# Turned features and attention weights in 512-byte pieces, with four blocks interleaved, in a graph-attention stack

## The chip, the core and the metric

The kernel runs on one core of one Trainium2 chip. The metric is the device time of one execution in microseconds (us); lower is better. The core has five engines that run side by side, each through its own list of instructions in order: TensorE (PE: matmuls, with weight loads shown as PEld), VectorE (DVE), ScalarE (ACT), GpSimd (POOL) and SyncE (SP), which here does nothing but issue transfers (DMAs). [...]

## What is computed

128 independent graphs of 128 nodes with 512 features each pass through four layers. Each layer adds a graph attention to its input and normalizes the rows. All arithmetic is float32. Cut to what matters here:

```python
# layer 1, for one graph: x is 128 x 512, mask is 128 x 128
def gat_layer(x, mask, W, a_src, a_dst, bias, concat):
    xl = (x @ W).reshape(B, N, H, F)
    asrc = jnp.einsum('bnhf,hf->bnh', xl, a_src)
    adst = jnp.einsum('bnhf,hf->bnh', xl, a_dst)
    e = jax.nn.leaky_relu(asrc[:, :, None, :] + adst[:, None, :, :], NEG_SLOPE)
    e = jnp.where(mask[..., None], e, NEG_INF)
    attn = jax.nn.softmax(e, axis=1)
    out = jnp.einsum('bsdh,bshf->bdhf', attn, xl)
    ...
h = elu(gat_layer(x, mask, W1, att_src1, att_dst1, b1, concat=True))    # 4 heads of 256
h = gat_layer(h, mask, W2, att_src2, att_dst2, b2, concat=False)        # 1 head of 512
x = layernorm(x + h)
```

Layer 0 mixes the rows with one head and no weight matrix. Layer 2 has a 512 x 512 weight matrix and 8 heads of 64. Layer 3 mixes with one head again.

## The kernel before

**The work of one graph.** The function `graph(g)` records one graph's work as some 170 operations (`Op`), each with an engine, an assumed cost, what it reads and what it writes. The nodes lie on the 128 partitions. TensorE contracts over partitions, so the features and the attention weights must be turned before it can take them.

**How something is turned (`turned`, lines 343 to 367).** VectorE transposes 32 x 32 blocks (line 348) into a buffer `zb`. One DMA writes it to a scratch tensor `scr` in memory (line 353). A second DMA reads it back so that the 32 x 32 blocks land on the right partitions. The count n says how many 128 x 128 blocks are turned at once: 4 for features of 512 and for four heads, 1 for a single head. In memory the order is block of 32 columns, then n, then 32 columns. There are two ways to read it back:

- With `moving=True` (line 358) each partition gets 4 pieces of n x 32 elements (512 bytes for n = 4). This is used for the four heads of layer 1 alone. Block h of the result is then four runs of 32 elements (the helper `parts`, line 532), and TensorE takes it as the moving operand (line 540).
- Otherwise (line 363) each partition gets 4 x n pieces of 32 elements, which is 128 bytes, so that each block is one run of 128 elements. TensorE takes it as the stationary operand, in a weight load: the features at line 453 (with `w1a` and with `wha`), two groups of four heads at line 585, and single heads at line 470.

Per graph there are five transfers of the kind n = 4 (features for layer 1, four heads of layer 1, features for layer 2, and the 8 heads of layer 2 in two groups) and three of the kind n = 1.

**TensorE's work in a graph.** Line 453 multiplies features by a weight matrix (`project`): 12 matmuls with 344 columns (`w1a`), 16 with 257 columns (`w2a`, whose stationary operand `hT` doesn't come from `turned`), and 8 with 264 columns (`wha`). Line 540 mixes the four heads of layer 1 in 8 matmuls, with the features as weights and the attention as moving operand. Line 585 mixes the 8 heads of layer 2, with the attention as weights and 64 columns streamed. Line 470 mixes a single head (3 times). Line 506 turns a mask.

**What sets the order.** `Pipeline.plan` is a planner that places the operations of one graph on a circle of `PERIOD = 24.7` us. For each operation it knows the assumed cost, an extra time until a transfer has landed, and latencies by engine (6 us for SP). It takes operations in the order of their earliest time, less 0.6 of the work that is left behind them, plus a random shift with a fixed seed, and places each at the first free time on its engine's circle. `Pipeline.run` then lays the same plan for all 128 graphs, one period apart, sorts everything by due time, and emits it. The times serve the order alone: [...] One graph's plan is some 18 periods long, so many graphs are in work at once. The planner also hands out buffers: all float32 buffers of 128, 512 or 1024 elements per partition come from common pools, with as many slots as the plan needs. The setup work (weights, their products with the attention vectors) is emitted among the first periods.

Of the kernel before, what the change touches and what calls it, by code (L numbers as in the profile page):

```python
# [16 lines left out]
P = 128  # L17
# [133 lines left out]
def tile_gat_stack(  # L151
# [25 lines left out]
    nc = tc.nc  # L177
    B, N, F = x.shape
    H1, FH = a1_src.shape
    HF = H1 * FH  # L180
    H2, FO = ah1.shape
# [48 lines left out]
    flat = "h f -> (h f)"  # L230
# [40 lines left out]
    for k in range(KF):  # L271
        for s in range(2):
            for h in range(H1):
                c, o = slice(h * FH, (h + 1) * FH), HF + s * H1 + h
# [39 lines left out]
    def graph(g):  # L314
        ops = []

        def op(engine, cost, emit, ins=(), outs=(), extra=0.0):
            ops.append(Op(engine, cost, emit, list(ins), list(outs), extra))
# [21 lines left out]
            ), [row], [db], 1.0 + 0.1 * nh)  # L340
            return db

        def turned(src, n, moving=False):

            zb, scr, out = Buf(f"zb{n}", [P, 4, n, 32]), Buf(f"scr{n}", [P, n * P]), Buf(f"pt{n}", [P, n, P])
            op("DVE", 0.12 + 0.133 * n, lambda: nc.vector.transpose(  # L348
                zb.ap.rearrange("p b h c -> p h b c"),
                src.ap.rearrange("p (h b c) -> p h b c", h=n, c=32) if len(src.shape) == 2  # L350
                else src.ap.rearrange("p h (b c) -> p h b c", c=32),
            ), [src], [zb])
            op("SP", 0.4, lambda: nc.sync.dma_start(
                out=scr.ap, in_=zb.ap.rearrange("p b h c -> p (b h c)")
            ), [zb], [scr], 0.2 * n)
            flat = lambda: scr.ap.rearrange("p f -> (p f)")
            if moving:
                op("SP", 0.6, lambda: nc.sync.dma_start(
                    out=out.ap.rearrange("p h i -> p (h i)").rearrange("p (q e) -> p q e", q=4),
                    in_=flat().rearrange("(q p e) -> p q e", q=4, p=P),  # L360
                ), [scr], [out], 1.0)
                return out
            op("SP", 0.65, lambda: nc.sync.dma_start(
                out=out.ap.rearrange("p h (q c) -> p h q c", q=4),
                in_=flat().rearrange("(q p h c) -> p h q c", q=4, p=P, h=n),
            ), [scr], [out], 1.5)
            return out

        class Col:
# [8 lines left out]
        def attend(db, h0, nh, src, mask, scaled=False):  # L378


            z, zz, nm, rs, ri = (Buf(f"{t}{nh}", s) for t, s in (
                ("z", [P, nh, P]), ("zz", [P, nh, P]), ("nm", [P, nh]), ("rs", [P, nh]),
                ("ri", [P, nh])))

            def prelu():
                for h in range(nh):
                    nc.scalar.activation(  # L387
                        z.ap[:, h, :], db.ap[:, h0 + h, :], AF.Prelu, bias=src(h0 + h), alpha=SLOPE
                    )

            def masked():
                for h in range(nh):
                    nc.vector.tensor_tensor_reduce(  # L395
                        out=zz.ap[:, h, :].rearrange("p (b a) -> p a b", b=4),
                        in0=z.ap[:, h, :].rearrange("p (a b) -> p a b", b=4),
                        in1=mask.ap.rearrange("p (a b) -> p a b", b=4), scale=-1.0, scalar=FMAX,
                        op0=ALU.add, op1=ALU.min, accum_out=nm.ap[:, h : h + 1],
                    )  # L400

            def exp():
                for h in range(nh):
                    nc.scalar.activation(  # L404
                        zz.ap[:, h, :], zz.ap[:, h, :], AF.Exp, bias=nm.ap[:, h : h + 1], scale=-1.0,
                        accum_out=rs.ap[:, h : h + 1],
                    )

            op("ACT", 0.08 + 0.293 * nh, prelu, [db, src.buf], [z])
            op("DVE", 0.08 + 0.225 * nh, masked, [z, mask], [zz, nm])  # L410
            op("ACT", 0.39 * nh, exp, [zz, nm], [zz, rs])
            op("DVE", 0.07, lambda: nc.vector.reciprocal(ri.ap, rs.ap), [rs], [ri])
            if scaled:
                op("POOL", 1.3, lambda: nc.gpsimd.tensor_mul(
                    zz.ap, zz.ap, ri.ap.unsqueeze(2).to_broadcast([P, nh, P])
                ), [zz, ri], [zz])
            return turned(zz, nh, moving=scaled), ri

        def norm(y, on_act=False):

# [23 lines left out]
        def project(xT, wa, nk, ncol, nchunk, t, evict):  # L444

            w = ncol // nchunk

            def chunk(c, ev):
                px = bank()
                cols = slice(c * w, (c + 1) * w)  # L450

                for k in range(nk):
                    op("PE", w * 4 / 2400 + 0.006, lambda k=k: nc.tensor.matmul(  # L453
                        px.ap[:, :w], lhsT=xT.ap[:, k, :], rhs=wa[:, k, cols],
                        start=(k == 0), stop=(k == nk - 1),
                    ), [xT] if k == 0 else [xT, px], [px])
                if ev == "DVE":
                    op("DVE", 0.11 + w / 960, lambda: nc.vector.tensor_copy(  # L458
                        t.ap[:, cols], px.ap[:, :w]), [px], [t])
                else:  # L460
                    op("ACT", 0.16 + w / 1200, lambda: nc.scalar.copy(  # L461
                        t.ap[:, cols], px.ap[:, :w]), [px], [t])

            for n, c in enumerate(reversed(range(nchunk))):
                chunk(c, evict[n])

        def mixed(pt, xv, width):

            pa = bank()
            op("PE", width * 4 / 2400, lambda: nc.tensor.matmul(  # L470
                pa.ap[:, :width], lhsT=pt.ap[:, 0, :], rhs=xv.ap[:, :width], start=True, stop=True
            ), [pt, xv], [pa])
            return pa

# [33 lines left out]
        pt, ri = attend(db, 0, 1, Col(sc0, 0, 1), m0)  # L508
        pa = mixed(pt, x0, F)
# [11 lines left out]
        xT = turned(x1, KF)  # L521
        xb = Buf("xb", [P, F])
        op("POOL", 1.25, lambda: nc.gpsimd.tensor_add(xb.ap, x1.ap, b2t), [x1], [xb])  # L523
        xl = Buf("xl1", [P, C1])
        project(xT, w1a, KF, C1, 3, xl, ["ACT"] * 3)
        db = spread(Col(xl, HF, H1), H1)
        pt, ri = attend(db, 0, H1, Col(xl, HF + H1, H1), m1, scaled=True)
# [1 line left out]

        e1, r1, hT = (Buf(t, [P, KH, P]) for t in ("e1", "r1", "hT"))  # L530

        def parts(b):
            return b.ap.rearrange("p h i -> p (h i)").rearrange("p (q h c) -> p q h c", q=4, h=H1)

        def block(c, pt=pt):
            pa = bank()

            for u in range(4):
                k = 4 * c + u
                op("PE", 0.225, lambda u=u, k=k: nc.tensor.matmul(  # L540
                    pa.ap[:, u * P : (u + 1) * P].rearrange("p (q c) -> p q c", q=4), lhsT=xl.ap[:, k * P : (k + 1) * P],
                    rhs=parts(pt)[:, :, k * P // FH, :], start=True, stop=True,
                ), [xl, pt, pa] if u else [xl, pt], [pa])
            half = lambda b: b.ap[:, 4 * c : 4 * c + 4, :].rearrange("p k i -> p (k i)")

            def biased(out, func):
                for u in range(4):
                    k = 4 * c + u
                    nc.scalar.activation(  # L549
                        out.ap[:, k, :], pa.ap[:, u * P : (u + 1) * P], func, bias=b1t[:, k : k + 1]  # L550
                    )

            op("ACT", 1.1, lambda: biased(e1, AF.Exp), [pa], [e1])
            op("ACT", 1.1, lambda: biased(r1, AF.Relu), [pa], [r1])
            op("DVE", 0.6, lambda: nc.vector.scalar_tensor_tensor(
                out=half(hT), in0=half(e1), scalar=-1.0, in1=half(r1), op0=ALU.add, op1=ALU.min
            ), [e1, r1], [hT])
# [8 lines left out]
        pt, ri = attend(db, 0, 1, Col(xl2, F + 1, 1), m1)  # L566
        pa = mixed(pt, xl2, F)
# [5 lines left out]
        xT = turned(x2, KF)  # L573
# [5 lines left out]
        def heads(q):  # L579
            pt, ri = attend(db, 4 * q, 4, Col(xl3, F + H2, H2), m2)  # L580
            pa = bank()

            for u in range(4):
                h = 4 * q + u
                op("PE", 0.225, lambda u=u, h=h: nc.tensor.matmul(  # L585
                    pa.ap[:, u * FO : (u + 1) * FO], lhsT=pt.ap[:, u, :],
                    rhs=xl3.ap[:, h * FO : (h + 1) * FO], start=True, stop=True,
                ), [pt, xl3, pa] if u else [pt, xl3], [pa])
            cols = slice(q * 4 * FO, (q + 1) * 4 * FO)
            op("DVE", 0.34, lambda: nc.vector.tensor_mul(  # L590
                x3.ap[:, cols].rearrange("p (h o) -> p h o", h=4),
                pa.ap[:, : 4 * FO].rearrange("p (h o) -> p h o", h=4),
                ri.ap.unsqueeze(2).to_broadcast([P, 4, FO]),
            ), [pa, ri], [x3])
# [11 lines left out]
        pt, ri = attend(db, 0, 1, Col(sc4, 0, 1), m3)  # L606
# [49 lines left out]
```

## Time and profile before

| what | us |
|---|---|
| median of 3 runs | 3197.62 (3196.52 to 3199.8) |
| the profiled execution | 3201.2 |
| its span, first to last instruction | 3199.3 |
| PE busy | 3073.7 (96%) |
| DVE busy | 3003.9 (94%) |
| ACT busy | 2444.6 (76%) |
| POOL busy | 1563.7 (49%) |

A group in the profile is one line, engine, operation and shape. Its columns are the count, the busy time in us and the mean ns of one, then the engine's idle time before it and who ended it. These groups are touched by the change:

```profile
L348 DVE STREAM_TRANSPOSE w<-w 128x512 f32<-128x512 f32 x640 | 446.0, 697 | 23.3 <-PE ps L540 9.1 <-PE ps L585 1.0 <-ACT w L435 1.0
L585 PEld LDWEIGHTS ps<-xl,w 128*128 128x128 f32 x2048 | 295.3, 197 | 104.2 <-issue 78.9 <-DVE mv L423 7.1 <-DVE sT L330 3.9
L585 PE MATMUL ps<-xl,w 128*128 128x64 f32 x2048 | 278.5, 271 | 25.4 <-DVE mv L423 9.9 <-DMA w<-scr 9.7 <-DVE sT L330 3.5
L540 PE MATMUL ps<-w,xl 128*128 128x128 f32 x2048 | 256.3, 278 | 0.1
L540 PEld LDWEIGHTS ps<-w,xl 128*128 128x128 f32 x2048 | 239.6, 192 | 0.8 <-ACT xl L461 0.3
```

The mean of one overlaps with its neighbours: the 12 passes of line 585 that follow each other begin far less than 271 ns apart. So the time that a kind of instruction takes from the engine is read from the distance between starts, or from the chain of waits, which gives each stretch to one owner.

The transfers, counted over the whole run:

```profile
DMA packets 1640373, 600.46 MB, mean 188 GB/s; under 512 B 1310464, under 2 KB 1490688, under 8 KB 1640016
q1 hardware_dynamic: 1636608, 589.44, 74.8%
```

The second line is the queue of SyncE's transfers: packets, MB, and the time that they took as a share of 16 DMA engines over the span.

### The profile page before, as it was taken

To read this page: it belongs to the slowest core of one execution; us is meant where nothing else is said; L and a number is where in the kernel's file an instruction comes from. 1 tells how busy PE (TensorE), PEld (TensorE's weight loads), DVE (VectorE), ACT (ScalarE), POOL (GpSimd) and SP (SyncE) were. 2 spreads that over 40 slices of the span, in tenths; PEclk is the share of its full clock that TensorE was granted. 3 is DMA by queue.
4 is the path that set the end of the run, shared out by engine and by line. 5 is a ranking of instruction groups with operands and counts; after the bars stand their busy time and mean duration, and the time that the engine had idled before them with its cause. 6 is when DMAs were issued, how large, how long until landed. Compare 5 with 4: busy or idle time off the path is not lost.

```text
span 3199.3 us, 60449 instructions
## 1 busy us (share of the span) xinstructions
PE 3073.7 (96%) x14212; PEld 2378.0 (74%) x14212; DVE 3003.9 (94%) x9976; ACT 2444.6 (76%) x8961; POOL 1563.7 (49%) x2328
## 2 busy tenths in 40 slices
PE   3999999999999999999999999999999999999974
PEld 1677777777777777777777777777777777777762
DVE  5768999999999999999999999999999999999885
ACT  1567888877878788788787887878878878788864
POOL 4334545555545455555455554545555545555334
PEclk9999999999999999999999999999999999999985
DMA  4467787777878777788787777777777787778774
GB/s 149 116 154 186 190 196 196 195 197 193 199 192 198 193 198 194 196 197 197 191 199 196 193 196 195 197 196 196 194 199 193 195 196 197 197 192 196 175 167 112
DMA packets 1640373, 600.46 MB, mean 188 GB/s; under 512 B 1310464, under 2 KB 1490688, under 8 KB 1640016
## 3 DMA queue, kind: packets, MB, share of 16 engines
q1 hardware_dynamic: 1636608, 589.44, 74.8%
q0 software_dynamic: 1936, 6.62, 0.6%
q8 instruction: 115, 1.88, 0.3%
q14 instruction: 242, 1.98, 0.2%
q10 hardware_dynamic: 1472, 0.53, 0.1%
HBM read 368.91 MB, written 227.48 MB: 186 GB/s over the span
## 4 chain that ended last, share of the span: by engine, by line
PE 93%; DVE 3%; DMA 2%; POOL 1%; ACT 1%; issue 1%; SPq 0%; ACTq 0%; POOLq 0%; DVEq 0%
PE ps L453 69%; PE ps L470 10%; PE ps L540 7%; PE ps L585 6%; DMA w<-scr 1%; DVE w L495 0%; PE ps L506 0%; DMA scr<-w 0%; ACT w L404 0%; DVE w L395 0%; DVE st L422 0%; DMA w_-1_4_139<-in_L_gnn_att_dst_dram 0%; POOL rd L427 0%; DVE w L348 0%; DVE w_-1_1_94 L266 0%
## 5 line engine op out<-in xcount | busy, mean ns | idle before, releaser
L453 PE MATMUL ps<-w2a,w 128*128 128x257 f32 x4096 | 953.2, 380 | 3.1 <-DVE xl L458 3.1
L453 PE MATMUL ps<-w1a,w 128*128 128x344 f32 x3072 | 917.2, 455 | 1.9 <-ACT w L549 0.9
L453 PEld LDWEIGHTS ps<-w2a,w 128*128 128x128 f32 x4096 | 758.3, 190 | 121.1 <-DVE xl L458 3.9
L453 PEld LDWEIGHTS ps<-w1a,w 128*128 128x128 f32 x3072 | 587.4, 191 | 348.6 <-issue 41.1
L404 ACT ACTIVATE w<-w,nm 128x128 f32<-128x128 f32 x1920 | 767.3, 412 | 31.9 <-DVE nm L395 26.6
L387 ACT ACTIVATE w<-w,xl 128x128 f32<-128x128 f32 x1664 | 543.5, 447 | 265.5 <-DVE w L513 239.6
L395 DVE CUSTOM_DVE_ANT_0 w<-w,w 128x128 f32<-128x128 f32 x1920 | 666.3, 456 | 24.7 <-ACT w L387 11.6
L549 ACT ACTIVATE w<-ps,b1t 128x128 f32<-128x128 f32 x2048 | 560.6, 404 | 112.3 <-PE ps L540 112.3
L348 DVE STREAM_TRANSPOSE w<-w 128x512 f32<-128x512 f32 (+1 forms) x1024 | 544.0, 541 | 32.3 <-PE ps L540 9.1
L426 POOL TENSOR_SCALAR rd<-mv 128x1 f32<-128x1 f32 x512 | 118.5, 232 | 920.5 <-DVE mv L423 894.3
L453 PEld LDWEIGHTS ps<-wha,w 128*128 128x128 f32 x2048 | 390.4, 191 | 121.4 <-issue 36.8
L453 PE MATMUL ps<-wha,w 128*128 128x264 f32 x2048 | 480.0, 388 | 0.0
L461 ACT COPY xl<-ps 128x344 f32<-128x344 f32 (+2 forms) x640 | 277.9, 435 | 175.3 <-PE ps L453 165.8
L404 ACT ACTIVATION_READ_ACCUMULATOR w<-w,nm 128x1 f32 x1920 | 401.2, 209 | 0.0
L523 POOL TENSOR_TENSOR w<-w,b2t 128x512 f32<-128x512 f32 x128 | 165.9, 1296 | 467.5 <-DVE w L348 282.0
L585 PEld LDWEIGHTS ps<-xl,w 128*128 128x128 f32 x2048 | 295.3, 197 | 104.2 <-issue 78.9
L422 DVE BATCH_NORM_STATS2 st<-w 128x6 f32<-128x512 f32 x512 | 353.9, 691 | 11.8 <-POOL w L614 7.3
L427 POOL TENSOR_TENSOR rd<-rd,neghalf 128x1 f32<-128x1 f32 x512 | 307.4, 600 | 42.7
L470 PE MATMUL ps<-w,w 128*128 128x512 f32 x512 | 281.7, 633 | 32.5 <-DMA w<-scr 16.1
L585 PE MATMUL ps<-xl,w 128*128 128x64 f32 x2048 | 278.5, 271 | 25.4 <-DVE mv L423 9.9
L395 DVE DVE_READ_ACCUMULATOR2_ANT nm<- 128x1 f32 x1920 | 291.4, 152 | 0.0
L495 DVE CUSTOM_DVE_ANT_0 w<-w,wf 128x512 f32<-128x512 f32 x256 | 282.2, 1103 | 0.0
(74 smaller groups left out, 3913.7 us busy)
## 6 DMA issues: line engine op xcount, KB each, us to landing
scr<-w SPq DMA_DIRECT2D x640, 256.0 KB
w<-scr SPq DMA_DIRECT2D x640, 256.0 KB
w<-row SPq DMA_DIRECT2D x128, 512.0 KB
w<-in_x_dram SPq DMA_DIRECT2D x128, 256.0 KB
w<-row SPq DMA_DIRECT2D x128, 256.0 KB
out_dram<-w SPq DMA_DIRECT2D x128, 256.0 KB
w<-row SPq DMA_DIRECT2D x384, 64.0 KB
scr<-w SPq DMA_DIRECT2D x384, 64.0 KB
```

Of the source, the lines that this page charges most:

```text
L348: op("DVE", 0.12 + 0.133 * n, lambda: nc.vector.transpose(zb.ap.rearrange("p b h c -> p h b c"), src.ap.rearrange("p (h b c) -> p h b c", ...
L387: nc.scalar.activation(z.ap[:, h, :], db.ap[:, h0 + h, :], AF.Prelu, bias=src(h0 + h), alpha=SLOPE)
L395: nc.vector.tensor_tensor_reduce(out=zz.ap[:, h, :].rearrange("p (b a) -> p a b", b=4), in0=z.ap[:, h, :].rearrange("p (a b) -> p a b", b= ...
L404: nc.scalar.activation(zz.ap[:, h, :], zz.ap[:, h, :], AF.Exp, bias=nm.ap[:, h : h + 1], scale=-1.0, accum_out=rs.ap[:, h : h + 1],)
L422: op("DVE", 0.6, lambda: nc.vector.bn_stats(st.ap, y.ap), [y], [st])
L427: nc.gpsimd.tensor_tensor(out=rd.ap, in0=rd.ap, in1=neghalf, op=ALU.pow)
L453: op("PE", w * 4 / 2400 + 0.006, lambda k=k: nc.tensor.matmul(px.ap[:, :w], lhsT=xT.ap[:, k, :], rhs=wa[:, k, cols], start=(k == 0), stop= ...
L461: op("ACT", 0.16 + w / 1200, lambda: nc.scalar.copy(t.ap[:, cols], px.ap[:, :w]), [px], [t])
L470: op("PE", width * 4 / 2400, lambda: nc.tensor.matmul(pa.ap[:, :width], lhsT=pt.ap[:, 0, :], rhs=xv.ap[:, :width], start=True, stop=True), ...
L495: op("DVE", 0.75, lambda: nc.vector.tensor_tensor_reduce(out=jk.ap, in0=xv.ap, in1=wv, scale=1.0, scalar=init, op0=ALU.mult, op1=ALU.add, ...
L549: nc.scalar.activation(out.ap[:, k, :], pa.ap[:, u * P : (u + 1) * P], func, bias=b1t[:, k : k + 1])
L585: op("PE", 0.225, lambda u=u, h=h: nc.tensor.matmul(pa.ap[:, u * FO : (u + 1) * FO], lhsT=pt.ap[:, u, :], rhs=xl3.ap[:, h * FO : (h + 1) * ...
```

## The change

There is one way to read back instead of two. VectorE writes the turned blocks so that the n blocks are interleaved: element c of block h lies at c x n + h. In memory the order is then block of 32 columns, column, n. Each partition reads 4 pieces of 32 x n elements, 512 bytes for n = 4, and holds the result as [128 columns, n]. So column i of block h lies 4 elements, which is 16 bytes, after column i - 1, and TensorE is given that step: as weights at lines 453 (features with `w1a` and `wha`) and 585, as moving operand at line 540. For n = 1 the layout stays as it was. The costs that the planner is told become those of the former `moving=True` for all read-backs: 0.6 instead of 0.65 on SP, and 1.0 instead of 1.5 until it has landed.

```diff
-        def turned(src, n, moving=False):
+        def turned(src, n):
...
-            zb, scr, out = Buf(f"zb{n}", [P, 4, n, 32]), Buf(f"scr{n}", [P, n * P]), Buf(f"pt{n}", [P, n, P])
+            zb, scr, out = Buf(f"zb{n}", [P, 4, 32, n]), Buf(f"scr{n}", [P, n * P]), Buf(f"pt{n}", [P, P, n])
             op("DVE", 0.12 + 0.133 * n, lambda: nc.vector.transpose(
-                zb.ap.rearrange("p b h c -> p h b c"),
+                zb.ap.rearrange("p b c h -> p h b c"),
...
             op("SP", 0.4, lambda: nc.sync.dma_start(
-                out=scr.ap, in_=zb.ap.rearrange("p b h c -> p (b h c)")
+                out=scr.ap, in_=zb.ap.rearrange("p b c h -> p (b c h)")
             ), [zb], [scr], 0.2 * n)
-            flat = lambda: scr.ap.rearrange("p f -> (p f)")
-            if moving:
-                op("SP", 0.6, lambda: nc.sync.dma_start(
-                    out=out.ap.rearrange("p h i -> p (h i)").rearrange("p (q e) -> p q e", q=4),
-                    in_=flat().rearrange("(q p e) -> p q e", q=4, p=P),
-                ), [scr], [out], 1.0)
-                return out
-            op("SP", 0.65, lambda: nc.sync.dma_start(
-                out=out.ap.rearrange("p h (q c) -> p h q c", q=4),
-                in_=flat().rearrange("(q p h c) -> p h q c", q=4, p=P, h=n),
-            ), [scr], [out], 1.5)
+            op("SP", 0.6, lambda: nc.sync.dma_start(
+                out=out.ap.rearrange("p i h -> p (i h)").rearrange("p (q e) -> p q e", q=4),
+                in_=scr.ap.rearrange("p f -> (p f)").rearrange("(q p e) -> p q e", q=4, p=P),
+            ), [scr], [out], 1.0)
             return out
...
-            return turned(zz, nh, moving=scaled), ri
+            return turned(zz, nh), ri
...
-                        px.ap[:, :w], lhsT=xT.ap[:, k, :], rhs=wa[:, k, cols],
+                        px.ap[:, :w], lhsT=xT.ap[:, k, :] if xT.shape[1] == nk else xT.ap[:, :, k], rhs=wa[:, k, cols],
...
-                pa.ap[:, :width], lhsT=pt.ap[:, 0, :], rhs=xv.ap[:, :width], start=True, stop=True
+                pa.ap[:, :width], lhsT=pt.ap[:, :, 0], rhs=xv.ap[:, :width], start=True, stop=True
...
-        def parts(b):
-            return b.ap.rearrange("p h i -> p (h i)").rearrange("p (q h c) -> p q h c", q=4, h=H1)
...
-                    pa.ap[:, u * P : (u + 1) * P].rearrange("p (q c) -> p q c", q=4), lhsT=xl.ap[:, k * P : (k + 1) * P],
-                    rhs=parts(pt)[:, :, k * P // FH, :], start=True, stop=True,
+                    pa.ap[:, u * P : (u + 1) * P], lhsT=xl.ap[:, k * P : (k + 1) * P],
+                    rhs=pt.ap[:, :, k * P // FH], start=True, stop=True,
...
-                    pa.ap[:, u * FO : (u + 1) * FO], lhsT=pt.ap[:, u, :],
+                    pa.ap[:, u * FO : (u + 1) * FO], lhsT=pt.ap[:, :, u],
```

## The prediction

> **What bounds the kernel now.** I read the busy times by stretch first, then the chain of waits in order of time, then the groups, then the timeline of VectorE and of the DMA queue. Busy time by stretch (columns: window; length; busy us and instruction count of PE, PEld, DVE, ACT, POOL; granted clock; DMA share; GB/s):
>
> ```profile
> 0.00:100.00 100.00, 41.46 (x106) 22.65 (x107) 55.37 (x202) 19.74 (x66) 39.34 (x62) 0.92 0.52 147
> 100.00:200.00 100.00, 95.89 (x412) 70.82 (x412) 65.70 (x199) 53.51 (x197) 33.35 (x48) 0.99 0.45 116
> 200.00:1600.00 1400.00, 1400.00 (x6564) 1091.43 (x6564) 1360.34 (x4520) 1119.22 (x4128) 697.68 (x1039) 1.00 0.79 194
> 1600.00:3000.00 1400.00, 1400.00 (x6583) 1092.33 (x6582) 1377.64 (x4554) 1127.10 (x4147) 714.79 (x1061) 1.00 0.79 196
> 3000.00:3100.00 100.00, 89.93 (x415) 71.22 (x414) 85.60 (x289) 75.85 (x279) 37.44 (x57) 0.91 0.70 167
> 3100.00:3200.00 100.00, 46.38 (x140) 29.56 (x138) 59.21 (x215) 49.14 (x150) 41.12 (x63) 0.61 0.51 120
> ```
>
> From 200 to 3000 us TensorE is busy without a gap, at full clock. Everything a faster transfer could win lies in the first 200 us (62.7 us of PE idle) and the last 200 us (63.7 us). "Busy" can hide waits when records overlap, so the chain must confirm it. One period of it, by line:
>
> ```profile
> 1600.75 0.17 PE ps L585 x2
> 1600.92 1.84 PE ps L540 x16
> 1602.76 0.87 PE ps L453 x4
> 1603.63 0.17 PE ps L585 x2
> 1603.80 0.11 PE ps L506
> 1603.91 3.04 PE ps L453 x14
> 1606.95 0.86 PE ps L470 x2
> 1607.81 1.28 PE ps L585 x12
> 1609.09 0.91 PE ps L470 x2
> 1610.01 3.56 PE ps L453 x16
> 1613.57 0.86 PE ps L470 x2
> 1614.42 9.97 PE ps L453 x38
> 1624.40 0.17 PE ps L585 x2
> 1624.57 1.84 PE ps L540 x16
> ```
>
> One graph takes 1624.57 - 1600.92 = 23.65 us, and the pieces follow without anything between. Each float32 matmul is two passes here (16 for the 8 heads at L585), and every pass has a weight load. Price of a pass: L453 with 257 columns 3.04/14 = 217 ns; with 264 columns 3.56/16 = 222 ns; with 344 columns (9.97 - 14 x 0.217)/24 = 289 ns; L470 with 512 columns 430 ns. These grow with the columns streamed, so the moving side sets them. L585 streams only 64 columns, yet takes 1.28/12 = 107 ns: there the weight load of 128 columns is the limit. L540 streams 128 columns and loads 128: 1.84/16 = 115 ns, both near the limit. 128 x 23.65 = 3027 us; the other 172 us of the span are fill and drain.
>
> [...] For a column step of exactly 16 bytes [...] No TensorE read in this trace has such a step, so the trace can't say. [...] The trace's packet records: 13.1 ns for 128 bytes, 29.7 ns for 512 bytes (median 27), so per byte the short ones are 1.8 times dearer.
>
> **The change part by part.**
> 1. Read-back. Of the 5 four-block transfers per graph, one (L358) was already in 512-byte pieces; 4 (L363: two feature turns, two halves of the heads) go from 2048 packets of 128 bytes to 512 packets of 512 bytes. Over 128 graphs 1,048,576 packets become 262,144: 1,048,576 x 13.1 / 16 = 859 us per DMA engine become 262,144 x 29.7 / 16 = 487 us, so the DMA share falls by 372/3199 = 0.12, to about 0.67 in the middle. One transfer: 128 x 13.1 = 1.7 us on each engine become 32 x 27 = 0.9 us. Its issue on SP falls from 629 ns (median of L363) to 384 ns (median of L358), 1.0 us per graph. In the middle all this is hidden behind TensorE: worth nothing. In fill and drain it counts where such a transfer ends a wait. The chain there names w<-scr for 4.9% of the first 200 us and 5.9% of the last 200 us, 21.6 us in all; single-block ones (unchanged in size) among them. The pieces that release L453 or L585 (3.83, 4.10, 3.56 us) are four-block; each loses 0.8 + 0.25 = 1.05 us, 3.2 us together. If all 21.6 us shrank by 1.05/3.8, it would be 6 us. The planner's own plan for one graph gets 2.0 us shorter (450.7 to 448.7). I take -5.5 us.
> 2. The planner. Its costs for SP drop (0.65 to 0.60, landing 1.5 to 1.0), so due times move for nearly all instructions and each engine's order changes. On TensorE the first five w2a matmuls move ahead of the layer-0 mix, one head (two passes) joins the run of six, and the other stays beside the mask transpose. Narrow passes cost one load each wherever they stand, except next to the transpose, and one pair still stands there: no change, to 0.05 us per graph either way.
> 3. Weights with a 16-byte step: the features at L453 with w1a (24 loads per graph) and with wha (16), and the heads at L585 (16). At L453 the load hides under 289 and 222 ns, so it may become 2.7 and 2.1 times as long before it costs. At L585 nothing hides it: every ns counts 16 times per graph, 2048 times in all. [...] Above: [...] (107 ns more), 16 x 0.107 = 1.7 us per graph, 218 us. I take nothing: [...] In the drain at half clock L585 takes 2.46/12 = 205 ns for the same load: the array's clock, not SBUF, paces it.
> 4. Moving operand with a 16-byte step: L540, 16 passes, now runs of 128 bytes. It has at most 115 - 107 = 8 ns of slack; bounds nothing to 16 x 0.1 = 1.6 us per graph, 205 us. I take nothing, for the same reason.
> 5. VectorE's transposes write with a 16-byte step (5 per graph, 697 ns each). VectorE is busy 23.35 of 23.65 us in this period, so only 0.3 us stand behind. The masking at L395 already writes with a 128-byte step, [...] In the timeline (start, us, engine, line):
>
> ```profile
> 1601.94 0.27 DVE L330 STREAM_TRANSPOSE w<-xl 128x128 f32<-128x128 f32 x1
> 1602.13 0.35 DVE L395 CUSTOM_DVE_ANT_0 w<-w,w 128x128 f32<-128x128 f32 x1
> 1602.34 0.14 DVE L395 DVE_READ_ACCUMULATOR2_ANT nm<- 128x1 f32 x1
> ```
>
> From start to start the contiguous 128-column transpose takes 0.19 us and the strided pass 0.21 us. So a stepped write costs at most 0.02 us per 128 columns: 5 x 4 x 0.02 = 0.4 us per graph above, nothing below. I take nothing; at the upper end the 0.3 us of cover are gone and 0.1 us x 128 = 13 us come out.
>
> No wait is added: each product still waits for the same transfer, now earlier. Sum on the profile's own time: 3199.3 - 5.5 = 3193.8 us of span (its execution took 3201.2 us with what lies around it; the median of the runs is 3197.62, 3.6 below). Against the median: 3192 us.
>
> **The rivals.** A measurement of this kernel can tell about 0.2% (6.4 us) from no change.
> A, hidden (0.64): TensorE stays the bound at 23.65 us per graph, only fill and drain shrink: 3192, from 3183 to 3203, since the new order in fill and drain may take or give some 5 us. For it: 2800 us without a gap, and 34.6 us of PE waits for w<-scr in all, an upper bound of what is to be had there.
> B, TensorE pays for the step (0.24): the slower rival. Place: L585, where the load has no cover, from the first ns; then L540 beyond 8 ns; then L453 wha beyond 2.1 times. A quarter slower on both: 16 x 27 + 16 x (134 - 115) ns = 0.74 us per graph, 95 us: 3192 + 95 = 3287. Twice on loads alone: 3192 + 218 = 3410. Twice on both (L540 at 214 ns, 203 us more): 3613. For it: [...] no such read in the trace. Against it: point 3, [...]
> C, VectorE becomes the bound (0.08): the new order puts other VectorE operations beside GpSimd's. At L395 one masking pass took 1.31 us instead of 0.35 where it fell beside a GpSimd addition; L495 with wf has a mean of 1103 against 667 ns with w0d. With 0.3 us of cover per graph, one more such meeting (1 us) costs 0.7 x 128 = 90 us: 3282; a third of one costs nothing. Against it: the same operations meet the same number of GpSimd operations, so gains are as likely as losses, and only losses above 0.3 us show.
> D, fill and drain shrink more (0.04): all 34.6 us of PE waits for w<-scr halve: 3180.
>
> **How the numbers follow.** The likeliest case is A, 3192. Within A, -5.5 us with some 6 us of scatter gives faster by over 0.2% in 45%, slower in 4%. Faster: 0.64 x 0.45 + 0.04 = 0.33. Slower: 0.24 + 0.08 + 0.03 = 0.35. Same: 0.32. The range runs from 3182 (D and A's low end nearly whole) to 3340, which takes in C and the mild half of B (up to about 40% slower reads) and leaves out doubled reads. A's own range is 3183 to 3203.
>
> **What would show it.** Right: in the middle PE busy again the whole stretch, a graph in 23.65 us, L585 at 107 ns and L540 at 112 to 115 ns per pass, weight loads with a mean of 190 ns everywhere, transposes of 512 columns near 697 ns, packets near 854,000 in all with some 262,000 under 512 bytes, DMA share near 0.67. Wrong by B: a longer mean of L585's loads against those of w2a (still contiguous), and a longer L585 or L540 in the chain. Wrong by C: PE idle in the middle, released by DVE. Wrong by D: the middle unchanged and the last 200 us clearly shorter.

## The result, and the profile after

The changed kernel takes 3676.04 us (median, 3675.42 to 3677.12) against 3198.71 us for the kernel before on the same chip. The ratio is 1.149, with a 95% interval from 1.147 to 1.151: slower by 477 us, where 3192 us were predicted, and 3340 at most. Line numbers in the changed kernel are lower: 453 became 446, 470 became 463, 506 became 499, 540 became 530, 585 became 575.

Busy time by stretch, in the changed kernel (columns as before: window; length; busy us and count of PE, PEld, DVE, ACT, POOL; granted clock; DMA share; GB/s):

```profile
200.00:1600.00 1400.00, 1400.00 (x5659) 1276.39 (x5658) 1127.75 (x3887) 961.06 (x3553) 601.13 (x891) 1.00 0.56 167
1600.00:3400.00 1800.00, 1800.00 (x7273) 1641.05 (x7273) 1464.84 (x5058) 1247.57 (x4586) 790.15 (x1178) 1.00 0.57 168
```

TensorE is still busy without a gap and at full clock, but in the same 1400 us it gets through 5659 passes where there were 6564. Its weight loads are busy for 1276 us where it was 1091. The other engines are less busy than before. VectorE, for one, stands idle for 123 us before its transposes of line 348, and TensorE's line 575 ends 111 us of that. So the passes themselves have become slower. The timeline of TensorE over one graph shows which (start us, us, what, count; where passes are merged into one row, the length takes in the end of the last one, so the time is read from start to start):

```profile
1612.90 3.79 PE L530 MATMUL ps<-w,xl 128*128 128x128 f32 x16
1616.51 3.65 PE L446 MATMUL ps<-w2a,w 128*128 128x257 f32 x16
1620.00 0.47 PE L575 MATMUL ps<-xl,w 128*128 128x64 f32 x2
1620.30 0.28 PE L499 MATMUL ps<-ident,w 128*128 128x128 f32 x1
1620.41 1.02 PE L463 MATMUL ps<-xl,w 128*128 128x512 f32 x2
1621.28 3.25 PE L575 MATMUL ps<-xl,w 128*128 128x64 f32 x14
1624.37 1.08 PE L463 MATMUL ps<-w,w 128*128 128x512 f32 x2
1625.28 3.90 PE L446 MATMUL ps<-wha,w 128*128 128x264 f32 x16
1629.02 2.33 PE L446 MATMUL ps<-w2a,w 128*128 128x257 f32 x10
1631.18 1.02 PE L463 MATMUL ps<-w,w 128*128 128x512 f32 x2
1632.04 7.10 PE L446 MATMUL ps<-w1a,w 128*128 128x344 f32 x24
1638.98 1.46 PE L446 MATMUL ps<-w2a,w 128*128 128x257 f32 x6
1640.28 3.82 PE L530 MATMUL ps<-w,xl 128*128 128x128 f32 x16
```

One graph takes 1640.28 - 1612.90 = 27.38 us instead of 23.65, which is 3.73 us more, and 128 x 3.73 = 477 us. By pieces:

- L530 (was L540): 1616.51 - 1612.90 = 3.61 us for 16 passes, 3.64 at the next graph. It was 1.84: +1.8 us.
- L575 (was L585): 0.30 us for the lone pair (one head's two passes, standing alone between other matmuls) and 1624.37 - 1621.28 = 3.09 us for the run of 14. It was 0.17 + 0.17 + 1.28 = 1.62: +1.77 us.
- L446 with wha: 1629.02 - 1625.28 = 3.74 us. It was 3.56: +0.18 us.
- L446 with w1a: 1638.98 - 1632.04 = 6.94 us for 24 passes, 289 ns each, as before. Its loads have the 16-byte step too, and cost nothing.

These are all four places where TensorE reads with the 16-byte step, and their sum, 3.75 us, is the whole loss within the rounding. The groups confirm it (count; busy us, mean ns of one; idle before):

```profile
L446 PEld LDWEIGHTS ps<-w1a,w 128*128 128x128 f32 x3072 | 893.6, 308 | 51.1 <-PE ps L446 28.1
L446 PEld LDWEIGHTS ps<-w2a,w 128*128 128x128 f32 x4096 | 782.2, 191 | 116.2 <-DVE xl L451 1.9
L575 PEld LDWEIGHTS ps<-xl,w 128*128 128x128 f32 x2048 | 507.2, 326 | 79.2 <-issue 50.8
L446 PEld LDWEIGHTS ps<-wha,w 128*128 128x128 f32 x2048 | 505.7, 323 | 55.8 <-DMA w<-row 26.6
```

The three groups of loads with the step have means of 308, 326 and 323 ns. Those of w2a, which still read contiguous columns, have 191. It is the sign that the prediction named for its rival B.

The transfers did what was said of them:

```profile
DMA packets 853940, 600.43 MB, mean 163 GB/s; under 512 B 261889, under 2 KB 704257, under 8 KB 853585
q1 hardware_dynamic: 850176, 589.44, 54.1%
```

Packets fell from 1,640,373 to 853,940, and the queue's share from 74.8% to 54.1%, of a longer span.

### The profile page after: what moved, and what is told of

It reads as the page before. It is cut to its first block, busy times and chain, and to the rows that moved or that the text cites. A ratio compares the mean times of both kernels' runs of the same rounds, so it can differ in the third digit from the quotient of the medians.

```text
span 3675.0 us, 60359 instructions
## 1 busy us (share of the span) xinstructions
PE 3552.7 (97%) x14212; PEld 3214.0 (87%) x14212; DVE 2907.5 (79%) x9976; ACT 2443.8 (66%) x8961; POOL 1564.1 (43%) x2328
## 2 busy tenths in 40 slices
DMA packets 853940, 600.43 MB, mean 163 GB/s; under 512 B 261889, under 2 KB 704257, under 8 KB 853585
## 3 DMA queue, kind: packets, MB, share of 16 engines
q1 hardware_dynamic: 850176, 589.44, 54.1%
q8 instruction: 114, 1.87, 0.2%
## 5 line engine op out<-in xcount | busy, mean ns | idle before, releaser
L446 PE MATMUL ps<-w2a,w 128*128 128x257 f32 x4096 | 953.4, 380 | 1.4 <-DVE xl L451 0.8
L446 PEld LDWEIGHTS ps<-w1a,w 128*128 128x128 f32 x3072 | 893.6, 308 | 51.1 <-PE ps L446 28.1
L446 PE MATMUL ps<-w1a,w 128*128 128x344 f32 x3072 | 912.5, 453 | 0.0
L348 DVE STREAM_TRANSPOSE w<-w 128x512 f32<-128x512 f32 (+1 forms) x1024 | 792.9, 804 | 123.2 <-PE ps L575 111.3
L446 PEld LDWEIGHTS ps<-w2a,w 128*128 128x128 f32 x4096 | 782.2, 191 | 116.2 <-DVE xl L451 1.9
L575 PEld LDWEIGHTS ps<-xl,w 128*128 128x128 f32 x2048 | 507.2, 326 | 79.2 <-issue 50.8
L388 DVE CUSTOM_DVE_ANT_0 w<-w,w 128x128 f32<-128x128 f32 x1920 | 543.2, 387 | 17.3 <-ACT w L380 14.6
L446 PEld LDWEIGHTS ps<-wha,w 128*128 128x128 f32 x2048 | 505.7, 323 | 55.8 <-DMA w<-row 26.6
L446 PE MATMUL ps<-wha,w 128*128 128x264 f32 x2048 | 513.2, 405 | 0.0
L575 PE MATMUL ps<-xl,w 128*128 128x64 f32 x2048 | 478.3, 378 | 25.7 <-DMA w<-scr 15.4
L530 PE MATMUL ps<-w,xl 128*128 128x128 f32 x2048 | 486.6, 405 | 0.0
L530 PEld LDWEIGHTS ps<-w,xl 128*128 128x128 f32 x2048 | 420.4, 205 | 43.5 <-issue 0.8
L451 DVE COPY xl<-ps 128x257 f32<-128x257 f32 (+1 forms) x256 | 109.9, 429 | 333.3 <-PE ps L446 333.2
L420 POOL TENSOR_TENSOR rd<-rd,neghalf 128x1 f32<-128x1 f32 x512 | 345.8, 675 | 42.6
```

The source lines that it names most:

```text
L348: op("DVE", 0.12 + 0.133 * n, lambda: nc.vector.transpose(zb.ap.rearrange("p b c h -> p h b c"), src.ap.rearrange("p (h b c) -> p h b c", ...
L388: nc.vector.tensor_tensor_reduce(out=zz.ap[:, h, :].rearrange("p (b a) -> p a b", b=4), in0=z.ap[:, h, :].rearrange("p (a b) -> p a b", b= ...
L420: nc.gpsimd.tensor_tensor(out=rd.ap, in0=rd.ap, in1=neghalf, op=ALU.pow)
L530: op("PE", 0.225, lambda u=u, k=k: nc.tensor.matmul(pa.ap[:, u * P : (u + 1) * P], lhsT=xl.ap[:, k * P : (k + 1) * P], rhs=pt.ap[:, :, k * ...
L575: op("PE", 0.225, lambda u=u, h=h: nc.tensor.matmul(pa.ap[:, u * FO : (u + 1) * FO], lhsT=pt.ap[:, :, u], rhs=xl3.ap[:, h * FO : (h + 1) * ...
```

## The experiments

All start from the kernel before and change one thing, or one group of reads, so each is compared with it on the same chip (3199.43, 3201.37 or 3200.81 us by the group of runs). Most of the reads can be given a step without touching the layout: the same buffer is read as if its blocks were interleaved. The product is then another one, and its time is what is asked for. A line in what follows is a stretch of 16 bytes of a partition, counted by what an operand touches; that the price goes by this count was a theory when the runs were put on record, and the steps of 8, 12, 16 and 32 bytes below are what bears on it. The helper for it adds five lines, so 453, 540 and 585 are called 458, 545 and 590 in these kernels:

```diff
+        def stepped(b, k, m):
+            flat = b.ap.rearrange("p h i -> p (h i)")
+            j = k // m * m * P
+            return flat[:, j : j + m * P].rearrange("p (i m) -> p i m", m=m)[:, :, k % m]
```

The first question was whether TensorE's reads cost the time at all, and which; layout, transfers, transposes and order stay as before in these four.

**Only the weight loads of the 8 heads (line 585), step 16 bytes.**

```diff
-                    pa.ap[:, u * FO : (u + 1) * FO], lhsT=pt.ap[:, u, :],
+                    pa.ap[:, u * FO : (u + 1) * FO], lhsT=stepped(pt, u, 4),
```

> The kernel before with one change: the weight loads of line 585 (16 passes per graph) step 16 bytes from column to column. Layout, transfers, VectorE and the planner's order stay as before; the loads pick other elements of the same buffer, so the products of layer 2's heads differ. Theory 'line' (each column a new 16-byte line, each read takes twice as long): a pass at L585 goes from 101 ns on average to about 212 ns, 16 x 0.111 x 128 = 227 us, 3425 us in all; mean of L585's weight loads from 197 to some 325 ns. Rival 'order' (the loss came from the new order of the engines): no change, 3198 us.

Measured: 3393.86 us, ratio 1.061 (1.059 to 1.062), +194 us. From the chain of waits in order of time (start us, us, owner):

```profile
1620.99 0.30 PE ps L590 x2
1621.29 1.84 PE ps L545 x16
...
1628.32 2.62 PE ps L590 x12
```

The 12 passes take 2.62 us instead of 1.28. In the records their starts are 233 ns apart where they were 112 (the first load of a run hides in part under the matmul ahead of it, so 2.62/12 = 218 ns comes out a little lower; in the changed kernel's trace the first load of the run of 14 starts at 1620.85 us, with the last pass of line 463, and its own matmul at 1621.28). L545, which reads contiguously here, keeps its 1.84 us. A graph takes 25.26 us (median), +1.61: 1.34 for the 12 and 0.13 for each lone pair. That is less than the 227 us expected for 16 equal passes, since a part of the longer load hides at the lone pairs (0.13 us where two loads grew by 2 x 0.121 = 0.24) and at the first load of the run (1.34 where twelve grew by 1.45).

**Only the moving operand of the 4-head mix (line 540), step 16 bytes.** The edit is `rhs=stepped(pt, k * P // FH, 4)` for `rhs=parts(pt)[:, :, k * P // FH, :]`; the output, the same 128 columns, is no longer named as four runs of 32.

> The kernel before with one change: the moving operand of line 540 (16 passes per graph) steps 16 bytes instead of taking runs of 128 bytes; it picks other elements of the same buffer, so layer 1's products differ. Theory 'line': a pass goes from 115 to about 226 ns, 16 x 0.111 x 128 = 227 us, 3425 us in all. Rival 'weights only' (only loads pay for the step, the moving side reads ahead): no change, 3198 us, and L540's slowness in the changed kernel is its neighbours' loads.

Measured: 3428.45 us, ratio 1.071 (1.070 to 1.073), +229 us. The chain:

```profile
1613.81 3.67 PE ps L545 x16
...
1622.52 1.28 PE ps L590 x12
```

16 passes take 3.67 us instead of 1.84, 229 ns each where it was 115, while L590 keeps its 1.28. Here a matmul streams a stepped operand, there a load takes one: the price is nearly the same (229 and 233 ns).

**Only the features (line 453 with w1a and wha), step 16 bytes.** The edit is `lhsT=xT.ap[:, k, :] if nk == KH else stepped(xT, k, 4)`.

> The kernel before with one change: the feature loads of line 453 with w1a (24) and wha (16) step 16 bytes; they pick other elements of the same buffer. Theory 'line': a load takes 225 to 235 ns; under 344 columns (289 ns) it stays hidden, under 264 columns (222 ns) it shows by 10 to 16 ns: 16 x 0.013 x 128 = 27 us, 3225 us. Rival 'order': 3198 us. A rival 'loads no longer overlap with matmuls when stepped': 40 x over 100 ns x 128, more than 3700 us.

Measured: 3222.13 us, ratio 1.007 (1.006 to 1.009), +23 us.

```profile
1616.43 3.73 PE ps L458 x16
...
1621.02 9.97 PE ps L458 x38
```

The 16 passes with wha take 3.73 us (it was 3.56), 233 ns each: the load is now longer than the 222 ns of streaming. The 38 passes with 24 of w1a in them take 9.97 us, to the hundredth what they took before: 233 ns of load lie hidden under 289 ns of streaming. 0.17 x 128 = 22 us.

**All three with a step of 8 bytes**, so that two elements fall on each 16-byte line (`stepped(..., 2)`).

> The kernel before with all three reads (loads of lines 453 and 585, moving operand of line 540) at a step of 8 bytes, two columns to a 16-byte line; they pick other elements of the same buffers. Theory 'line' [...]: as before, 3198 us, passes of L585 near 107 ns and of L540 near 115 ns. Rival 'any step' (a stepped column costs in proportion to the lines fetched): half of the loss of 16 bytes, about 3198 + 240 = 3440 us, or the whole of it, 3670 us.

Measured: 3211.04 us, ratio 1.004 (1.003 to 1.005), +12 us.

```profile
1606.70 1.87 PE ps L545 x16
...
1613.62 1.35 PE ps L590 x12
...
1615.89 3.56 PE ps L458 x16
```

L590 takes 1.35 us (118 ns from start to start), L545 1.87, wha its old 3.56; the 0.07 and 0.03 us more per graph are the 12 us. So a step of 8 bytes is nearly free (118 ns where it was 112), and one of 16 is not (233). That fits a price for each line. It doesn't yet exclude that only the step counts, in some other way. Two more sizes were tried for that.

**Loads of line 585 with a step of 12 bytes.** 128 columns then touch 96 lines: four elements on three lines.

```diff
-                    pa.ap[:, u * FO : (u + 1) * FO], lhsT=pt.ap[:, u, :],
+                    pa.ap[:, u * FO : (u + 1) * FO], lhsT=pt.ap.rearrange("p h i -> p (h i)")[:, : 3 * P].rearrange("p (i m) -> p i m", m=3)[:, :, u % 3],
```

> The kernel before with one change: line 585's weight loads step 12 bytes, so 128 columns lie in 96 lines of 16 bytes; they pick other elements of the buffer. Theory 'a line costs 1.82 ns' (233 ns for 128 lines): a load takes 96 x 1.82 = 175 ns, a pass that stands in a run 175 ns from start to start; the mean over all passes 149 to 156 instead of 101 ns, 16 x 0.05 x 128 = 100 to 115 us: 3300 to 3315 us. Rival 'half rate as soon as less than two columns share a line': 233 ns, 3394 us, as with 16 bytes.

Measured: 3297.88 us, ratio 1.030 (1.029 to 1.032), +97 us.

```profile
1601.76 0.23 PE ps L585 x2
...
1606.00 1.97 PE ps L585 x12
```

From start to start 173 to 177 ns.

**Loads of line 540 with a step of 32 bytes**, 128 lines, every second one skipped (`lhsT=xl.ap[:, :HF].rearrange("p (i m) -> p i m", m=8)[:, :, k]`):

> The kernel before with one change: line 540's weight loads (of the features, 16 passes per graph) step 32 bytes; they pick other elements of the same buffer. Theory 'a line costs 1.82 ns': 128 lines as with 16 bytes, 233 ns per pass instead of 115 ns, 16 x 0.117 x 128 = 240 us: 3440 us. Rival 'the cost grows with the step': over 300 ns per pass, more than 3580 us.

Measured: 3449.82 us, ratio 1.078 (1.076 to 1.080), +249 us.

```profile
1623.61 3.86 PE ps L540 x16
```

Starts lie 238 to 240 ns apart, about what 16 bytes cost the loads of line 585.

The sizes together, as distance between the starts of passes that the load of 128 columns limits (line 585, or 590 with the helper; the last row is line 540, which also streams 128 columns):

| step | lines touched | ns per pass | ns per line |
|---|---|---|---|
| 4 bytes | 32 | 112 | (3.5) |
| 8 bytes | 64 | 118 | 1.84 |
| 12 bytes | 96 | 175 | 1.82 |
| 16 bytes | 128 | 233 | 1.82 |
| 32 bytes | 128 | 238 | 1.86 |

For these loads of 128 float32 columns at full clock, the time is the larger of two: 112 ns for the columns, and about 1.82 ns for each 16-byte line. At 8 bytes the two just meet (64 x 1.82 = 116 ns, measured 118). From 12 to 16 bytes the time grows with the step, by 14.6 ns per byte of it (175/12 and 233/16). The 238 ns at 32 bytes are what 238/14.6 = 16.3 bytes would cost, so by this estimate the rise ends near 16 bytes. That fits a price for each 16-byte line and not one for the distance. How the memory is built isn't shown.

The next four runs took the other parts of the change alone.

**Only VectorE's transposes writing with the 16-byte step** (`zb.ap.rearrange("p b h c -> p (b h c)").rearrange("p (b c h) -> p h b c", b=4, h=n)` as the output view; what is read back is then in another order).

> The kernel before with one change: VectorE's transposes of four blocks write with a 16-byte step (the blocks interleaved); transfers, TensorE's reads and the order stay as before, so turned features and weights have their columns in another order. Theory 'VectorE pays': from start to start a transpose goes from 0.622 to 0.948 us, as in the changed kernel; 5 x 0.33 = 1.6 us per graph against a cover of 0.3 us that shows and at most 0.7 us more hidden in overlapping records: VectorE becomes the bound, 3199 + (1.6 - 0.3 to 1.0) x 128 = 3280 to 3370 us. Rival 'the transposes were slow in the changed kernel because of TensorE's reads': 697 ns each as before, 3199 us.

Measured: 3227.72 us, ratio 1.008 (1.007 to 1.010), +26 us. That is well below the 3280 us at which its theory began; the reason follows with the groups.

**Only the masking pass of line 395 with a 16-byte step on its output** (`b=32` for `b=4` in its three views), where before it has 128 bytes:

> The kernel before with one change: the masking passes of line 395 write with a 16-byte step, 32 elements before the next round over the same lines, instead of a 128-byte step with 4 elements before the next round; the attention's columns get another order. Theory 'a line must be written again soon': the pass goes from 0.23 us (start to start) to about 0.31 us, 15 x 0.08 = 1.2 us per graph, of which 0.3 to 1.0 us are covered: 3225 to 3315 us. Rival 'only transposes pay for stepped writes': 0.23 us, 3199 us.

Measured: 3199.77 us, ratio 0.9995 (0.9986 to 1.0003): no change. The groups of VectorE between 800 and 2600 us, of the run with stepped transposes, then of the run with the other step in the masking, then of the kernel before:

```profile
L348 DVE STREAM_TRANSPOSE w<-w 128x512 f32<-128x512 f32 x378 | 418.9, 1108 | 6.8
L395 DVE CUSTOM_DVE_ANT_0 w<-w,w 128x128 f32<-128x128 f32 x1130 | 323.4, 398 | 0.0
```

```profile
L395 DVE CUSTOM_DVE_ANT_0 w<-w,w 128x128 f32<-128x128 f32 x1141 | 405.9, 471 | 0.0
L348 DVE STREAM_TRANSPOSE w<-w 128x512 f32<-128x512 f32 x382 | 265.7, 696 | 6.9
```

```profile
L395 DVE CUSTOM_DVE_ANT_0 w<-w,w 128x128 f32<-128x128 f32 x1140 | 402.2, 463 | 0.0
```

A transpose of 512 columns goes from 696 to 1108 ns (622 to 950 ns from start to start: +0.33 us). So the transpose does pay. The masking pass has 471 ns where it had 463, with 240 against 231 ns from start to start: a step of 16 bytes costs it hardly more than one of 128. With both steps each element lies on another line, and no run has this pass with a contiguous output, so whether it pays for a step at all isn't shown. The prediction's reference for the transpose, this pass against a contiguous transpose, compared two different instructions and was no measure of what a step costs.

Five transposes add 5 x 0.33 = 1.6 us per graph, yet a graph takes only 0.19 us more, 24 us in all. VectorE's idle time didn't give the rest: it is busy 1777 of these 1800 us in both kernels. Its other instructions have become shorter while its transposes grew. The masking pass has a mean of 398 ns instead of the 463 of the kernel before, which for 15 passes is about 1.0 us per graph. Why they could become shorter isn't shown.

**Only the 512-byte pieces on the read-back** (the transfer of line 363 takes the views of line 358):

> The kernel before with one change: all four-block read-backs come in 512-byte pieces (lines of 32 columns of four blocks stay side by side, so TensorE's runs of 128 take parts of four blocks); order, VectorE and TensorE's reads as before. It is the transfer part of the change alone. Theory of the prediction: the middle keeps its 23.65 us per graph, fill and drain shrink by 3 to 6 us: 3193 to 3196 us, DMA share in the middle from 0.79 to 0.67. Rival 'fill and drain don't wait for these': 3199 us. Rival 'transfers disturb TensorE': PE passes get shorter, below 3180 us.

Measured: 3198.38 us, ratio 0.9988 (0.9981 to 0.9994), some 3 to 4 us faster.

**Only the planner's costs** (0.6 and 1.0 for 0.65 and 1.5):

> The kernel before with one change: the planner is told the changed kernel's costs of a read-back (0.6 and 1.0 instead of 0.65 and 1.5), so every engine gets the changed kernel's order; all layouts and transfers as before. Theory 'order is neutral': within 6 us of before, 3193 to 3205 us. Rival 'the order carries the part of the loss that the three reads don't explain' (477 less 194 + 229 + 23 = 31 us): 3230 us.

Measured: 3203.69 us, ratio 1.0009 (1.0001 to 1.0017), 2 to 3 us slower. Busy time between 200 and 1600 us of both, the first that of the 512-byte pieces:

```profile
200.00:1600.00 1400.00, 1400.00 (x6564) 1091.46 (x6563) 1360.71 (x4526) 1119.00 (x4130) 699.28 (x1038) 1.00 0.64 194
```

```profile
200.00:1600.00 1400.00, 1400.00 (x6565) 1091.16 (x6564) 1209.01 (x4539) 1119.34 (x4129) 748.01 (x1039) 1.00 0.79 194
```

The pieces take the DMA share from 0.79 to 0.64 and TensorE gets not one pass more done: 6564, as in the kernel before. The new order leaves TensorE as it was too, and VectorE falls from 1360 to 1209 us busy, from 97% to 86%.

Then the question whether the parts add up. **All three reads with 16 bytes, and before's order, transfers and transposes:**

> The kernel before with all three reads (loads of lines 453 and 585, moving operand of line 540) at a step of 16 bytes, and nothing else of the change: the planner's order, VectorE's writes and the transfers stay as before; the reads pick other elements of the same buffers. Theory 'sum': 3199 + 194 + 229 + 23 = 3645 us, some 30 us below the changed kernel, which then owes the rest to its order and ramps. Rival 'the reads hinder each other': 3675 us from the reads alone.

Measured: 3651.19 us, ratio 1.141 (1.139 to 1.142), +450 us. The three alone gave 194 + 229 + 23 = 446: they add. The changed kernel lost 477. Of this 27 us remain, in which the gain of the pieces and the loss of the planner's costs (each some 3 us) cancel. The chain of this run:

```profile
1607.78 0.30 PE ps L590 x2
1608.09 3.67 PE ps L545 x16
...
1612.62 0.30 PE ps L590 x2
...
1616.94 2.62 PE ps L590 x12
```

A graph takes 27.26 us here and 27.39 in the changed kernel (medians). In before's order two heads stand as lone pairs between wider matmuls, at 0.30 us each. In the changed order one of them stands in the run, which grows from 2.62 us for 12 to 3.09 for 14: 0.47 us for two passes. So a lone pair hides 0.17 us of its loads that a pair in the run doesn't; 0.13 us of it remain in the graph's time, 128 x 0.13 = 16 us. This is read from the two traces; no run has the stepped reads and the new order without the rest. Of what is left, six single graphs in the changed kernel's trace take longer than the others, five of them by 1.6 us and some 550 to 580 us apart, in all 9 us; in this run there are three, in all 3.4 us. That makes another 5 us. What lengthens those graphs stays open (in those of 1.6 us the time is lost in the wha passes and just ahead of them, 5.2 us for wha instead of 3.7). The last 6 us are no more than the half-width of the changed kernel's interval.

Last, what can be kept of the change at no cost: **only the features of layer 1 interleaved**, with the 512-byte read-back and the stepped transpose, planner's costs as before. All the computation is kept.

```diff
-        def turned(src, n, moving=False):
+        def turned(src, n, moving=False, mixed=False):
...
+            if mixed:
+                op("SP", 0.65, lambda: nc.sync.dma_start(
+                    out=out.ap.rearrange("p i h -> p (i h)").rearrange("p (q e) -> p q e", q=4),
+                    in_=flat().rearrange("(q p e) -> p q e", q=4, p=P),
+                ), [scr], [out], 1.5)
+                return out
...
-                        px.ap[:, :w], lhsT=xT.ap[:, k, :], rhs=wa[:, k, cols],
+                        px.ap[:, :w], lhsT=xT.ap[:, k, :] if xT.shape[1] == nk else xT.ap[:, :, k], rhs=wa[:, k, cols],
...
-        xT = turned(x1, KF)
+        xT = turned(x1, KF, mixed=True)
```

> A kernel with the reference's output: only the features of layer 1 are interleaved and read back in 512-byte pieces (line 453 with w1a, loads under 344 streamed columns); everything else, the planner's costs too, as before. Theory 'a line costs 1.82 ns': the loads take 233 ns under passes of 289 ns, TensorE's 23.65 us per graph stay; one transpose of five is 0.33 us longer, about what VectorE's 0.3 us of cover hold: 3195 to 3208 us, no gain from the shorter transfer that can be told. Rival 'a stepped load costs even when it is hidden' : 24 passes longer by 10 ns or more, over 3230 us.

Measured: 3200.05 us, ratio 0.9997 (0.9989 to 1.0005): no change. The stepped loads (under 289 ns of w1a) and one slower transpose of five are hidden, and so is the gain: the DMA share between 200 and 1600 us is 0.76 instead of 0.79, and TensorE gets through 6564 passes there, as before. No version of the change that keeps the computation beat the kernel before; the 512-byte pieces alone, some 3 us faster, give other products.

## Why the prediction was wrong, point by point

What bounds the kernel was read rightly: TensorE, pass by pass, with L585 limited by its load (112 to 233 ns with its load's step) and L540 near both limits (115 to 229 ns with a step on its moving operand, to 238 to 240 with one on its load). It is why a dearer read went straight into the time. The pieces of rival B stood at the right places: L585 grew by 121 ns a pass, L540 by 114, wha by 11, and w1a stayed hidden at 289. B at "twice on both" was 3613 us. Its sum of 421 us for the reads was close to the 450 measured, but in part by luck, for its errors have both signs: L585 cost 194 us and not 218, since a load grew by 121 ns (233 against 112) rather than 107 but hid in part; L540 cost 229 and not 203; and wha, whose load of 233 ns passed the 222 ns of streaming, added 23.

- **Step 3 failed (weights with a 16-byte step, taken at nothing).** The argument let the stepped read keep the contiguous one's pace, one float32 column in some 0.85 ns, with another line for each column. That was the author's estimate; the trace held no such read. The runs show 1.82 ns per line, more than twice that. A contiguous load touches a line every 112/32 = 3.5 ns. With the 16-byte step it would have to touch one every 112/128 = 0.87 ns to take no longer, and it was measured at half that pace. Measured alone: +194 us at L585 and +23 us at L453, where +0 was taken. The upper bound of 218 us for L585 was near the truth, but it came from a load grown by 107 ns, an estimate that no trace showed, where it grew by 121, and with its cover left out.
- **Its second argument failed as well.** In the drain at half clock, L585 took 205 ns for its load, and that was read as "the array's clock, not SBUF, paces it". This is right of a contiguous read and says nothing of a stepped one. The changed kernel's own drain shows the difference. Busy time by stretch (its granted clock is the third number from the end, 0.50) and TensorE's timeline there:

```profile
3600.00:3604.00 4.00, 3.76 (x13) 3.30 (x14) 1.83 (x5) 0.40 (x1) 1.53 (x3) 0.50 0.91 296
```

```profile
3600.24 3.04 PE L575 MATMUL ps<-xl,w 128*128 128x64 f32 x12 [7.46 <-DMA w<-scr]
3603.07 2.02 PE L463 MATMUL ps<-w,w 128*128 128x512 f32 x2
```

  (3603.07 - 3600.24)/12 = 236 ns per pass at half clock, with the first load in the open; 233 ns at full clock. From start to start inside the run it is 233 ns at both clocks, so the read with the 16-byte step didn't follow the granted clock. The contiguous one did: 1.28/12 = 107 ns at full clock, 205 at half; from start to start, 112 and 213. The run with a step of 12 bytes has both limits in one kernel. Below is a run of 12 passes from the drain of the kernel before, then one from the drain of that kernel, both at a granted clock of 0.50:

```profile
3092.75 2.66 PE L585 MATMUL ps<-xl,w 128*128 128x64 f32 x12
3095.20 2.02 PE L470 MATMUL ps<-w,w 128*128 128x512 f32 x2
```

```profile
3190.27 2.66 PE L585 MATMUL ps<-xl,w 128*128 128x64 f32 x12
3192.73 2.02 PE L470 MATMUL ps<-w,w 128*128 128x512 f32 x2
```

  At full clock the 12-byte step takes 173 to 177 ns where the contiguous load takes 112: the lines are the limit. At half clock it takes (3192.73 - 3190.27)/12 = 205 ns, as the contiguous load does with (3095.20 - 3092.75)/12 = 204: the columns are. At half clock the columns hide the price of these 96 lines. So the reading of a contiguous load at half clock could say nothing of it, and the profile before held no read that the lines limited.
- **Step 4 failed for the same reason (moving operand, taken at nothing).** +229 us alone. The upper bound of 205 us was too low: a pass grew by 114 ns (229 against 115), where at most 100 were allowed.
- **Step 5 failed, with little consequence.** "At most 0.02 us per 128 columns" became 0.08 us (0.33 per 512). Its evidence set the masking pass beside a contiguous transpose, another instruction. In the changed kernel it is hidden, because TensorE's graph is 3.7 us longer (VectorE is busy 1128 us of 1400 there); alone it costs 26 us.
- **Step 1 held.** Packets 853,940 against some 854,000; under 512 bytes 261,889 against 262,000. With the pieces alone: DMA share 0.64 against 0.67, and 3 to 4 us gained against 5.5. In the middle it is hidden, as said. In that run's chain w<-scr takes 3.3% of the first 200 us and 4.2% of the stretch from 3000 to 3200 us, 15.0 us where it was 21.6.
- **Step 2 held for the kernel as it was and not for the change as a whole.** With contiguous loads the new order is neutral (+0.09%). "Narrow passes cost one load each wherever they stand" isn't so with stepped loads: a lone pair between wide matmuls takes 0.30 us and a pair in the run 0.47, 16 us by the two traces. The two steps were costed apart, and this cost lies between them.
- **Rival C went the other way:** the new order took 151 us of 1400 off VectorE's busy time.

The trace before held no TensorE read with a 16-byte step, so no row of it decided between A and B. A chance of 0.24 for B was then too little, and the range should have reached to the doubled read.

## What to carry to other kernels

Before a layout is changed for the sake of a transfer, count the 16-byte lines that each TensorE operand touches: here a read of 128 float32 columns at full clock took the larger of about 0.87 ns per column and 1.82 ns per line. Two columns on a line took 118 ns and one column on a line 233, where contiguous columns took 112. Other counts of columns and other types were not measured. The load of 233 ns cost nothing under a matmul that streams for 289 ns, 11 ns under one of 222, and 121 ns in a run of passes where the load itself set the pace. And transfers that TensorE didn't wait for in the middle of the run bought next to nothing when they were made cheaper: 15 points of DMA share gave 0.12%.

## What was not expected of the hardware

- The price of a read with a 16-byte step was the same at both clocks seen: 233 ns from start to start at a granted clock of 0.50 and at 1.00, whereas the contiguous load takes 213 and 112 ns. At half clock the step cost 20 ns and not 121.
- Weight loads and a moving operand paid nearly the same for a line (233 and 229 ns for 128), and loads with a step of 32 bytes cost hardly more (238, at line 540) than those with 16 (233, at line 585).
- A VectorE transpose paid for a 16-byte step on its output (696 to 1108 ns for 512 columns). For the masking pass it hardly mattered whether the step was 128 or 16 bytes (463 and 471 ns).
- VectorE's busy time was no fixed sum of work: the order alone changed it from 1360 to 1209 us in 1400, with the same instructions and the same speed of the whole.
